# A reordered head, and float32 rows added by GpSimd's indirect transfers for nine batches of the last level of a graph layer on Trainium2

## The chip, the cores and the metric

One Trainium2 chip, one of its cores. The metric is the device time of one execution in microseconds; of several executions the median is given. The profile is of one execution, taken by the hardware profiler.

## The reference

A layer norm with a rectifier, one message-passing layer over a graph, and a residual. There are 12500 nodes with 64 features and 212500 edges that are sorted by destination; the hidden width is 128.

```python
    h = jnp.maximum(_layernorm(x, axis=-1), 0.0)
    ...
        edge_in = jnp.concatenate([h[row], h[col], dist], axis=1)
        e = jax.nn.silu(edge_in @ eW1 + eb1)
        e = jax.nn.silu(e @ eW2 + eb2)
        agg = jax.ops.segment_sum(e, row, num_segments=h.shape[0])
        node_in = jnp.concatenate([h, agg], axis=1)
        out = jax.nn.silu(node_in @ nW1 + nb1) @ nW2 + nb2
```

`row` is the source of an edge (and the node that it is summed into), `col` its destination, `dist` its weight. The layer's output is added to x.

## The kernel before, in words

A node is l * 100 + b: l is its place (0 to 124), b its bucket (0 to 99). The first edge matrix is split: A holds h times the part for the source, B the part for the destination, so the first layer of an edge is A[source] + B[destination] + weight and bias. A and B are kept as two float32r halves side by side (256 numbers, `ta` and `tb` in DRAM), whose sum is the float32 row.

**Sorting.** The edges come in 208 blocks of 1024 in the order of destination. For each block DVE counts the edges by source bucket (`oh` L457, `each` L465, `terms` L481, `rank` L483, and `pick` L446, which selects rows of B), TensorE forms the rows Q = B[destination] + weight + bias (`qp` L531), ACT copies them with the source's place in its bucket (`qs`, L543 and L546), and GpSimd sends them by eight indirect transfers a block (L553) to their bucket and rank in the DRAM buffer `q`. Slots of `q` that may stay empty are filled with zeros beforehand on ACT's queue (L123).

**Levels.** The ranks are cut into 14 levels; a level begins when the block that fills it has been sent. A level has 25 batches of four buckets, and a batch has one or two steps of 512 slots; the last level has one step a batch. A batch's Q rows come by one load on SP (`qt`, L612; four buffers), its A rows by another (`a`, L632; three buffers, 512 KB).

One step passes through these stages, in a loop over `turn` that takes a different step at each place: `one` (L719, DVE: which node of its bucket a slot belongs to), `lr` and `oneT` (L668 on TensorE and L673 on ACT: its transpose), `pt` (L685: transposes of the Q rows; L692: eight products of oneT with A's halves, which pick A's row for each slot and add it), `e` (L701, ACT), `p` (L730, L736, L740: second layer), `seg` (L753: sum by node), and the addition to `aggT` (L762 or L764, DVE). Between the stages, at the places marked None (hooks), other work is let in: sorting of later blocks, making of A, the node stage.

**Level 0** makes A itself, in a generator `made_a` that is advanced one part at each hook, three batches ahead: load of h (`hrl`, L642), product (L288, ACT L292, DVE L295), store to `ta` (L647), and h's share of the node stage: `zo` (L651), `zos` (L654, ACT; one buffer), stored to `own` (L656).

**Last level.** Once a batch's sum is complete, the node stage for its buckets is interleaved with the steps of later batches: x rows (`xr`, L335, the addition on GpSimd), `misc` (L348, on top of the own share), `zs` (L349), `o` (L358), `os` (L361), and the own share of the next batch copied into `misc` (L363).

**Order.** TensorE, DVE, ACT and SP run their instructions in the order of the program; GpSimd's order is planned by the scheduler. The head (the first 30 us) is a list of calls to generators: `src0` turns the sources of the first half into place and bucket, `lists_` the destinations into window starts, `rows_` and `made[0]` the norm and the first rows of B, `firstw` the edge weights.

Of the kernel before, what the change touches and what calls it, by code (L numbers as in the profile page):

```python
# [28 lines left out]
F32 = mybir.dt.float32  # L29
# [3 lines left out]
I32 = mybir.dt.int32  # L33
# [6 lines left out]
P = 128  # L40
# [39 lines left out]
def tile_gnn(ctx: ExitStack, tc: tile.TileContext, x, src, dst, ew, eW1, eb1, eW2, eb2, nW1, nb1, nW2, nb2, out):  # L80
# [194 lines left out]

    tb0 = dram.tile([P * NE, 2 * H], F32, name="tb0")
    tb00 = dram.tile([P * G, 2 * H], F32, name="tb00")
    ta_buckets, tb_buckets = (t.rearrange("(l b) f -> l b f", b=NB) for t in (ta, tb))

    def product(s, hr, ps, tag, to):  # L280
# [93 lines left out]
    with work:  # L374
# [38 lines left out]
        def load(s):  # L413

            if s < nblocks:
                p, g = s // 2, s % 2
                win = wins[p % NW]
                table, end = (tb0, NE * P) if s < EARLY else (tb, NB * P)
                if s < 2 * FIRST_PAIRS:
                    table, end = tb00, G * P  # L420
                assert s < EARLY or len(done_b) == NB // G
                if g == 0:
                    of = identb[:, p % HB :: HB][:, :, None].to_broadcast([P, 2, HB])
                    nc.scalar.copy(sels[p % NW].rearrange("p (a m) -> p a m", a=2), of)
# [180 lines left out]
        def fetch(i):  # L605
            if i >= len(batches):
                return
            c, B, n = batches[i]
            assert not any(pending[: c + 1])
            at = B * G * ROWS + G * (ENDS[c] - n * P)  # L610
            qt = ld2.tile([P, G * most, W], F32, name="qt")
            ins = nc.sync.dma_start(  # L612
                qt[:, : G * n, :].rearrange("p j w -> p (j w)"),
                q[at : at + G * n * P, :].rearrange("(p j) w -> p (j w)", p=P),
            ).ins
            for later in range(c + 1, len(LEVELS)):
                tc.declare_no_dep(ins, group=f"rows{later}", reason="these ranks were full before")
            tc.add_manual_dep(ins, last_rows[LEVELS[c][1] - 1].name, AFTER)
            tc.add_to_no_dep_group("loads", ins)
            batch[c, B] = [qt, None, None]  # L620

        def fetch_a(i):

            if i >= len(batches):
                return
            c, B, n = batches[i]
            a = lda.tile([P, G, 2 * H], F32, name="a")
            if c == 0:
                making[B] = made_a(B, a)
                next(making[B])  # L630
            else:
                nc.sync.dma_start(a, ta_buckets[:, B * G : B * G + G])  # L632
            batch[c, B][1] = a
# [3 lines left out]
        def made_a(B, a):  # L637

            while B not in done_b:
                next(feed)  # L640
            hr = late.tile([P, G // 2, P], F32, name="hrl")
            nc.sync.dma_start(hr, hd[:, B * G // 2 : (B + 1) * G // 2, :])  # L642
            for _ in range(3):
                yield
            yield from product(0, hr, mm, "mm", a.rearrange("p g (k h) -> p g k h", k=2))
            yield
            nc.sync.dma_start(ta_buckets[:, B * G : B * G + G], a)  # L647
            zo = [mm.tile([P, G // 2, L], F32, name="zo", tag="mm") for _ in range(2)]
            for h in range(2):
                half = slice(h * D, (h + 1) * D)  # L650
                nc.tensor.matmul(zo[h], w1n[half, :], hr[half, :, :L], start=True, stop=True)  # L651
            zos = late1.tile([P, G * L], F32, name="zos")
            for h in range(2):
                nc.scalar.copy(zos.rearrange("p (i a l) -> p i a l", a=2, l=L)[:, :, h], zo[h])  # L654
            yield
            nc.sync.dma_start(own[:, B, :], zos)  # L656
            yield

        def of(k):
# [2 lines left out]
            return batch[c, B], [((g * G + t) % n * G + (g * G + t) // n, (g * G + t) // n) for t in range(G)]  # L662

        def s_turn(k):
            tops = st[k]["one"].rearrange("p g l -> p (g l)").bitcast(BF16)
            lr = mm.tile([L, G, P], F32, name="lr", tag="mm")
            for t in range(G):
                nc.tensor.matmul(lr[:, t, :], tops[:, 2 * t * L + 1 : 2 * (t + 1) * L : 2], identb, start=True, stop=True)  # L668
            st[k]["lr"] = lr

        def s_one_t(k):
            oneT = wk.tile([L, G, P], F32, name="oneT")
            nc.scalar.copy(halves(oneT), st[k].pop("lr"))  # L673
            st[k]["oneT"] = oneT

        def s_pt(k):

            (qt, a, _), tiles = of(k)
            c, B, _, _ = steps[k]
            for _ in making.pop(B, ()) if c == 0 else ():  # L680
                pass
            oneT = st[k].pop("oneT")
            pt = mm.tile([P, G, P], F32, name="pt", tag="mm")
            for t, (j, _) in enumerate(tiles):
                nc.tensor.matmul(  # L685
                    pt[:, t, :], qt[:, j, :H], ident, is_transpose=True, start=t == 0, stop=False, skip_group_check=True
                )
            for b, same in itertools.groupby(range(G), lambda t: tiles[t][1]):
                same = list(same)
                cols = slice(same[0], same[-1] + 1)  # L690
                for i in range(2):
                    nc.tensor.matmul(  # L692
                        pt[:, cols, :],
                        halves(a[:L, b, i * H : (i + 1) * H]),
                        halves(oneT[:, cols, :]),
                        start=False,
                        stop=i == 1,
                        skip_group_check=True,
                    )
            e1 = wk.tile([P, G, P], F32, name="e1")  # L700
            nc.scalar.activation(e1, pt, AF.Silu)  # L701
# [257 lines left out]
        with listing:  # L959
# [5 lines left out]
            consts, zone_ = tables(), zones()  # L965
            next(rows_)
            next(consts)
            next(lists_)
            limits()
            next(rows_)  # L970
            next(firstw)
            next(lists_)
            nc.scalar.copy(halves(three2[:, 0, :]), three)
            nc.gpsimd.tensor_tensor(three2[:, 1, :], three, three2[:, 0, :], op=OP.subtract)
            last_rows_of(wins[0])
# [2 lines left out]
                last_rows_of(win)  # L978
            for xs in xss:
                nc.gpsimd.memset(xs, 0.0)  # L980
            next(rows_)
            next(src0)
            next(lists_)
            next(made[0])
            for part_ in (src0, made[0], firstw, made[0], made[0], lists_, src0, consts):
                next(part_)
            load_rows(0)
            load(0)
            load_sources(1)
            load(1)  # L990
            for part_ in (lists_, zone_):
                next(part_)
# [29 lines left out]
        aggT = aggp.tile([P, NB, L], F32, name="aggT")  # L1022
        late = work.enter_context(tc.tile_pool(name="late", bufs=3))
        late1 = work.enter_context(tc.tile_pool(name="late1", bufs=1))
        ld2 = work.enter_context(tc.tile_pool(name="ld2", bufs=NQ))
        lda = work.enter_context(tc.tile_pool(name="lda", bufs=NA))
        ones_ = work.enter_context(tc.tile_pool(name="ones", bufs=NO))
# [202 lines left out]
```

## Time and profile before

| | |
|---|---|
| median of 3 runs | 3503.77 us (3501.37 to 3517.39) |
| the profiled execution | 3483.84 us |
| its span | 3482.0 us |
| mean granted TensorE clock | 0.802 |
| first send (L553) | at 27.02 us |
| level 0, first and last fetch | 283.64 and 526.44 us |
| busy: TensorE, DVE, ACT, GpSimd | 67%, 53%, 40%, 47% |

A row of the timeline gives start, duration, engine, line, operation, output<-inputs, shape, number of instructions, and in brackets how long the engine had been idle before and what ended it. PE is TensorE, PEld its weight loads, POOL is GpSimd, and SPq the queue of SP. In the groups of the page, the numbers behind the count are busy time, mean nanoseconds of one, and idle time ahead of them by releaser. The chain of waits has start, duration, engine and line only.

### The profile page before, as it was taken

Reading aid. Unit: us, or ns where it says so; the run is one execution under the profiler, and the core shown is the slowest. Engines: PE = TensorE matmul, PEld = TensorE weight load, DVE = VectorE, ACT = ScalarE, POOL = GpSimd, SP = SyncE. Lnnn points to the kernel's source line nnn. Section 1 sums busy time; section 2 is a strip of 40 time slices with the busy share of each in tenths; the row PEclk is TensorE's granted clock in tenths of the full one; section 3 lists DMA queues with packets and bytes.
Section 4 is the critical chain, followed back from the end, with each engine's and each line's share of the span. In section 5 each row is a group of like instructions: output and inputs, shape, how many; then the busy total and the mean of one; then the engine's idle time right before and its main releaser. Section 6 shows DMA issues by size and latency. Waiting matters only on the chain. (4 is left out here: it accounts for less than half of the span.)

```text
span 3482.0 us, 47653 instructions
## 1 busy us (share of the span) xinstructions
PE 2344.1 (67%) x16730; PEld 2160.0 (62%) x16772; DVE 1842.7 (53%) x2884; ACT 1380.4 (40%) x3001; POOL 1641.7 (47%) x1724
## 2 busy tenths in 40 slices
PE   4445777735776567656765676767777767776799
PEld 3234666634665567556755666766676766766797
DVE  8775566554546445544454444455554554555443
ACT  3223444322444344334433444434443434443454
POOL 7665555465445544444445444444444544444401
PEclk7555778866887788778877888888888888888899
DMA  4344566654544345445553445455555655555586
GB/s 153 136 162 165 174 203 213 196 165 144 175 147 155 130 137 169 137 133 157 170 169 130 146 163 161 145 160 165 171 169 152 186 163 163 172 175 158 164 260 188
DMA packets 243744, 572.56 MB, mean 164 GB/s; under 512 B 47069, under 2 KB 106133, under 8 KB 243191
## 3 DMA queue, kind: packets, MB, share of 16 engines
q1 hardware_dynamic: 160308, 393.28, 36.6%
q0 software_dynamic: 53408, 122.68, 9.8%
q10 hardware_dynamic: 29782, 53.47, 4.8%
q8 instruction: 136, 2.23, 0.3%
q14 instruction: 110, 0.90, 0.1%
HBM read 349.93 MB, written 219.27 MB: 163 GB/s over the span
## 5 line engine op out<-in xcount | busy, mean ns | idle before, releaser
L553 POOL DMA_INDIRECT q<-qs,to x1661 | 1604.8, 966 | 1672.4 <-ACT qs L546 1174.1
L692 PE MATMUL pt<-oneT,a 125*128 125x128 f32 (+1 forms) x2800 | 491.9, 320 | 621.3 <-ACT oneT L673 518.8
L692 PEld LDWEIGHTS pt<-oneT,a 125*128 125x128 f32 x2800 | 415.3, 222 | 667.8 <-ACT oneT L673 552.5
L701 ACT ACTIVATE e<-pt 128x512 f32<-128x512 f32 x450 | 268.9, 598 | 1087.3 <-PE pt L692 374.4
L764 DVE TENSOR_TENSOR aggT<-aggT,seg 128x500 f32<-128x500 f32 x324 | 218.3, 674 | 876.0 <-remote 266.0
L736 PE MATMUL p<-w,e 128*128 128x128 f32 x3600 | 597.1, 319 | 0.0
L753 PE MATMUL seg<-one,e 128*128 128x125 f32 x3592 | 557.8, 303 | 51.1 <-DVE aggT L764 32.8
L736 PEld LDWEIGHTS p<-w,e 128*128 128x128 f32 x3600 | 548.1, 230 | 24.3 <-issue 22.4
L753 PEld LDWEIGHTS seg<-one,e 128*128 128x128 f32 x3592 | 498.1, 213 | 69.7 <-DVE aggT L764 37.9
L531 PE MATMUL qp<-win,pick 128*128 128x256 f32 x1664 | 379.4, 363 | 101.0 <-issue 49.2
L719 DVE TENSOR_TENSOR one<-misc,qt 128x500 f32<-128x500 f32 x425 | 286.0, 673 | 288.7 <-remote 75.4
L531 PEld LDWEIGHTS qp<-win,pick 128*128 128x128 f32 x1664 | 299.6, 248 | 184.1 <-issue 85.0
L543 ACT COPY qs<-qp 128x512 f32<-128x512 f32 x418 | 245.5, 588 | 406.4 <-issue 147.2
L740 ACT ACTIVATE e<-p 128x512 f32<-128x512 f32 x450 | 268.9, 598 | 278.8 <-remote 151.4
L465 DVE TENSOR_REDUCE each<-oh 128x100 bf16<-128x800 bf16 x208 | 318.3, 1530 | 7.2
L673 ACT CAST oneT<-lr 125x512 fp32r<-125x512 f32 x450 | 263.8, 586 | 101.8 <-remote 49.2
L685 PE MATMUL pt<-ident,qt 128*128 128x128 f32 x1800 | 284.8, 282 | 11.4 <-issue 5.0
L481 DVE TENSOR_TENSOR terms<-oh,misc 128x800 f32<-128x800 bf16 x208 | 203.6, 979 | 128.2 <-remote 95.4
L730 ACT COPY p<-b2f 128x512 f32<-128x512 f32 x450 | 267.1, 593 | 0.0
L685 PEld LDWEIGHTS pt<-ident,qt 128*128 128x128 f32 x1800 | 220.6, 147 | 28.5 <-issue 12.9
L483 DVE TENSOR_REDUCE rank<-terms 128x8 f32<-128x864 f32 x208 | 219.0, 1053 | 7.2
L668 PEld LDWEIGHTS <-one 128*125 128x125 bf16 x1800 | 197.5, 161 | 28.4 <-issue 27.0
(163 smaller groups left out, 1736.7 us busy)
## 6 DMA issues: line engine op xcount, KB each, us to landing
a<-ta SPq DMA_DIRECT2D x325, 512.0 KB
qt<-q SPq DMA_DIRECT2D x250, 288.0 KB
qt<-q SPq DMA_DIRECT2D x100, 576.0 KB
q<-zeros ACTq DMA_DIRECT2D x25, 1080.0 KB
q<-qs,to POOLq DMA_INDIRECT x1661
win<-tb SPq DMA_DIRECT2D x208, 120.0 KB
tb<-got SPq DMA_DIRECT2D x30, 512.0 KB
q<-zeros ACTq DMA_DIRECT2D x20, 720.0 KB
```

Source lines behind the costliest of these rows:

```text
L465: nc.vector.tensor_reduce(each, oh.rearrange("p t b -> p b t"), AX.X, OP.add)
L531: nc.tensor.matmul(qp[:, t % 2, :k], halves(pick[:, t * P : (t + 1) * P]), halves(win[:, :k, v]), start=v == 0, stop=v == 1,)
L553: ins = nc.gpsimd.indirect_dma_start(out=q[:], out_offset=bass.IndirectOffsetOnAxis(ap=to[:k, j : j + 1], axis=0), in_=qs[:k, t % 2, a, :] ...
L673: nc.scalar.copy(halves(oneT), st[k].pop("lr"))
L685: nc.tensor.matmul(pt[:, t, :], qt[:, j, :H], ident, is_transpose=True, start=t == 0, stop=False, skip_group_check=True)
L692: nc.tensor.matmul(pt[:, cols, :], halves(a[:L, b, i * H : (i + 1) * H]), halves(oneT[:, cols, :]), start=False, stop=i == 1, skip_group_c ...
L701: nc.scalar.activation(e1, pt, AF.Silu)
L719: nc.vector.tensor_tensor(one.rearrange("p (b j) l -> p b j l", j=n), (spots if c < len(LEVELS) - 1 else nodes1)[:, None, None, :].to_broa ...
L730: nc.scalar.copy(p2, b2f)
L736: nc.tensor.matmul(p2[:, t, :], e1[:, t, :], w2, start=False, stop=t == G - 1, skip_group_check=True)
L740: nc.scalar.activation(e2, p2, AF.Silu)
L753: nc.tensor.matmul(item[2][:, b, :], e2[:, t, :], one[:, t, :], start=j < G, stop=j >= G * (n - 1))
```

## The change

Lines are counted in the new kernel here, so some stand up to 37 lines further down.

**Level 0.** Behind the own store, `made_a` gets one more part: the float32 sum of A's halves is formed on DVE in `a32` and stored to a new DRAM buffer `ta32`. `a32` takes the same single buffer as `zos`.

**Last level.** For the batches whose number is a multiple of three (0, 3, ... 24: 9 of 25), A's rows come from `ta32`: GpSimd works out the row number of each slot's source (an empty slot takes some row, and is not summed), and four indirect transfers, one for each of the batch's tiles, add the rows of 128 slots onto Q's rows in `qt`. For these batches there is no load of A, no `lr`, no `oneT`, and no product L692; `pt` is the transposes alone.

**Head.** Same work, other order: the norm first, then the sources of the first half, the first rows of B, the destinations. The loads of the second half's sources are issued ahead of the first window's.

```diff
+            if picked_up(c, B):
+                near = wk.tile([P, G], F32, name="near")
+                nc.gpsimd.tensor_scalar(near, qt[:, :G, H], 1.0, float(NB), op0=OP.max, op1=OP.mult)
+                row_of = wk.tile([P, G], I32, name="row_of")
+                nc.gpsimd.tensor_tensor(near, near, shift[:, B * G : B * G + G], op=OP.add)
+                nc.gpsimd.tensor_copy(row_of, near)
+                for t in range(G):
+                    nc.gpsimd.indirect_dma_start(
+                        out=qt[:, t, :H],
+                        out_offset=None,
+                        in_=ta32[:],
+                        in_offset=bass.IndirectOffsetOnAxis(ap=row_of[:, t : t + 1], axis=0),
+                        compute_op=OP.add,
+                    )
+
+        def picked_up(c, B):
+
+            return c == len(LEVELS) - 1 and B % 3 == 0
...
             c, B, n = batches[i]
+            if picked_up(c, B):
+                return
             a = lda.tile([P, G, 2 * H], F32, name="a")
...
-            zos = late1.tile([P, G * L], F32, name="zos")
+            zos = late1.tile([P, G * H], F32, name="zos", tag="zos")[:, : G * L]
...
             nc.sync.dma_start(own[:, B, :], zos)
             yield
+            a32 = late1.tile([P, G, H], F32, name="a32", tag="zos")
+            nc.vector.tensor_tensor(a32, a[:, :, :H], a[:, :, H:], op=OP.add)
+            nc.sync.dma_start(ta32.rearrange("(l b) f -> l b f", b=NB)[:, B * G : B * G + G, :], a32)
+            yield
...
         def s_turn(k):
+            if picked_up(*steps[k][:2]):
+                return
...
         def s_one_t(k):
+            if picked_up(*steps[k][:2]):
+                return
...
-            for b, same in itertools.groupby(range(G), lambda t: tiles[t][1]):
+            for b, same in itertools.groupby(range(G), lambda t: tiles[t][1]) if oneT is not None else ():
...
-            next(lists_)
             limits()
             next(rows_)
+            next(rows_)
+            next(src0)
+            next(made[0])
+            next(lists_)
             next(firstw)
-            next(lists_)
...
-            next(rows_)
-            next(src0)
-            next(lists_)
             next(made[0])
-            for part_ in (src0, made[0], firstw, made[0], made[0], lists_, src0, consts):
+            for part_ in (src0, lists_, lists_, made[0], made[0], firstw, src0, lists_, consts):
                 next(part_)
             load_rows(0)
+            load_sources(1)
             load(0)
-            load_sources(1)
...
+        shift = aggp.tile([P, NB], F32, name="shift")
+        nc.vector.tensor_scalar(shift, nodes1[:, :NB], -float(NB + 1), None, op0=OP.add)
```

DVE's order in level 0 after the change, where the first three batches' `zos` have been stored (a tile's number tells its instances apart; `a_2170`, `a_2175` and `a_2180` are the A rows of batches 0, 1 and 2):

```order
L486 TENSOR_SCALAR to_2324<-rank_2322 128x8
L754 TENSOR_TENSOR one_2350<-misc_211,qt_2173 128x500
L458 TENSOR_TENSOR oh_2377<-misc_211,bkt_178 128x800
L466 TENSOR_REDUCE each_2379<-oh_2377 128x100
L680 TENSOR_TENSOR a32_2383<-a_2170 128x512
L680 TENSOR_TENSOR a32_2386<-a_2175 128x512
L680 TENSOR_TENSOR a32_2389<-a_2180 128x512
L447 TENSOR_SCALAR pick_2252<-bc_2381,same_148,extra0_152 128x512
L477 TENSOR_TENSOR alike_2428<-bkt_178 128x64
```

Before, `pick_2252` stood right behind `each`; the three additions now stand between them. The other 22 stand singly.

GpSimd's order at the end of the sends, after the change (the first two rows are the last sends of the program, then come batches 0, 3 and 6 of the last level):

```order
L554 DMA q_62<-qs_28132,to_28090 230528x144 x3
L554 DMA q_62<-qs_28177,to_28090 230528x144 x2
L624 TENSOR_SCALAR near_28618<-qt_28616 128x4
L626 TENSOR_TENSOR near_28618<-near_28618,shift_1030 128x4
L627 COPY row_of_28620<-near_28618 128x4
L629 DMA qt_28616<-ta32_175,row_of_28620 128x128 x4
L624 TENSOR_SCALAR near_28711<-qt_28709 128x4
L626 TENSOR_TENSOR near_28711<-near_28711,shift_1030 128x4
L627 COPY row_of_28713<-near_28711 128x4
L629 DMA qt_28709<-ta32_175,row_of_28713 128x128 x4
L336 TENSOR_TENSOR xr_28745<-xr_28745,nb2b_185 125x256
L336 TENSOR_TENSOR xr_28791<-xr_28791,nb2b_185 125x256
```

Before, the `xr` additions followed the last sends; two batches' gathers now stand ahead of them, and from there on one batch's gathers stand ahead of every three additions.

ACT's order in the head, of before and then of after (`x0` is the squared norm input, `var` the root, `sf` the sources, `got` the first rows of B):

```order
L787 ACTIVATE x0_77<-cen_217 128x256
L875 COPY firstf_221<-dstR_79 128x1
L792 ACTIVATE var_229<-var_229 128x4
L914 COPY ew00_127<-ew0_126 8x512
L973 COPY three2_125<-three_124 3x128
L896 COPY sf_80<-srcR_78 104x1024
L886 COPY base_i_179<-lot_236 1x64
L806 COPY hr_260<-ht_257 128x256
L292 COPY got_265<-ab_266 128x2x128
```

```order
L822 ACTIVATE x0_77<-cen_218 128x256
L827 ACTIVATE var_226<-var_226 128x4
L931 COPY sf_80<-srcR_78 104x1024
L841 COPY hr_236<-ht_233 128x256
L910 COPY firstf_238<-dstR_79 128x1
L949 COPY ew00_127<-ew0_126 8x512
L1010 COPY three2_125<-three_124 3x128
L293 COPY got_256<-ab_257 128x2x128
L293 COPY got_256<-ab_260 128x2x128
```

The root, the sources and `hr` moved ahead of the copies that wait for the destinations and the edge weights.

More of the change, by code (lines that the diff above doesn't have):

```diff
@@ L277, in tile_gnn @@
     tb00 = dram.tile([P * G, 2 * H], F32, name="tb00")
+    ta32 = dram.tile([P * NB, H], F32, name="ta32")
     ta_buckets, tb_buckets = (t.rearrange("(l b) f -> l b f", b=NB) for t in (ta, tb))
@@ L681, in s_pt @@
                 pass
-            oneT = st[k].pop("oneT")
+            oneT = st[k].pop("oneT", None)
             pt = mm.tile([P, G, P], F32, name="pt", tag="mm")
@@ L685, in s_pt @@
                 nc.tensor.matmul(
-                    pt[:, t, :], qt[:, j, :H], ident, is_transpose=True, start=t == 0, stop=False, skip_group_check=True
+                    pt[:, t, :],
+                    qt[:, j, :H],
+                    ident,
+                    is_transpose=True,
+                    start=t == 0,
+                    stop=oneT is None and t == G - 1,
+                    skip_group_check=True,
                 )
-            for b, same in itertools.groupby(range(G), lambda t: tiles[t][1]):
+            for b, same in itertools.groupby(range(G), lambda t: tiles[t][1]) if oneT is not None else ():
                 same = list(same)
```

## Prediction

> **What bounds the kernel now.** I read the page first, then the windows of 100 us, then the chain of waits, and the timeline at the three places that the change touches. The first rows are of the page.
>
> ```profile
> PE 2344.1 (67%) x16730; PEld 2160.0 (62%) x16772; DVE 1842.7 (53%) x2884; ACT 1380.4 (40%) x3001; POOL 1641.7 (47%) x1724
> ...
> L553 POOL DMA_INDIRECT q<-qs,to x1661 | 1604.8, 966 | 1672.4 <-ACT qs L546 1174.1
> ...
> L764 DVE TENSOR_TENSOR aggT<-aggT,seg 128x500 f32<-128x500 f32 x324 | 218.3, 674 | 876.0 <-remote 266.0
> ```
>
> No engine is full over the span, so the stages have to be read apart. The windows show, for each stretch, the busy microseconds of PE, its weight loads, DVE, ACT and POOL, then the granted clock and the share of the DMA engines.
>
> ```profile
> 300.00:400.00 100.00, 73.42 (x425) 61.77 (x423) 52.83 (x85) 39.00 (x98) 50.50 (x54) 0.70 0.50 171
> 700.00:800.00 100.00, 32.62 (x157) 26.24 (x158) 49.59 (x76) 17.75 (x47) 65.14 (x68) 0.57 0.43 139
> 3300.00:3400.00 100.00, 99.92 (x870) 94.53 (x870) 40.39 (x67) 57.84 (x107) 8.77 (x12) 1.00 0.82 257
> 3340.00:3350.00 10.00, 10.00 (x97) 10.00 (x96) 4.14 (x6) 6.04 (x13) 1.46 (x2) 1.00 1.01 339
> ```
>
> There are three kinds of stage. In level 0 (300 to 400 us) all engines are between 39% and 73%: they wait for each other in program order. At 700 to 800 us PE is at 33%, waiting for rows. In the last level, from about 3340 us, PE has no idle time and runs at the full granted clock; there a microsecond of PE removed can be a microsecond of time. The chain of waits is PE alone there; one step of it, 5.20 us, is
>
> ```profile
> 3453.93 0.94 PE seg L753 x8
> 3454.88 0.44 PE pt L685 x4
> 3455.31 0.84 PE pt L692 x8
> 3456.16 0.89 PE misc L348 x2
> 3457.05 0.89 PE p L736 x8
> 3457.94 0.96 PE o L358 x8
> 3458.90 0.24 PE lr L668 x4
> ```
>
> **The change, part by part: the last level.** For 9 of 25 batches `pt L692` (0.84) and `lr L668` (0.24) go: 1.08 us each, 9.7 us at most. But the `misc L348` behind them needs DVE's sum of the seg just made. At the end of the span, where neither pt nor lr stands between, the timeline shows how much of the gap remains:
>
> ```profile
> 3463.95 1.11 PE L753 MATMUL seg<-one,e 128*128 128x125 f32 x8
> ...
> 3465.85 0.69 PE L348 MATMUL misc<-aggT,w1g 128*128 128x500 f32 x1 [0.79 <-DVE aggT L764]
> ```
>
> From seg to misc it is 1.90 us there and 2.23 us (3453.93 to 3456.16) in the normal step. So of the 0.84 only 0.33 is gained and the rest becomes PE's wait for DVE; the 0.24 of lr stands elsewhere and is gained whole: 0.57 per batch, about 5 us for nine. The matching removals on ACT (nine `oneT` copies) and SP (nine loads) are worth nothing, as neither ends the chain.
>
> Against it stands the new chain: fetch of qt, three small POOL operations, four gathers, landing, then PE's transposes. How much time there is between a fetch and its transposes:
>
> ```profile
> 4.99 0.53 POOL L170 TENSOR_SCALAR low<-nodes 128x100 f32<-128x100 f32 x1
> ...
> 3328.26 2.47 SPq L612 DMA_DIRECT2D qt<-q  x2
> ...
> 3337.22 0.32 SPq L612 DMA_DIRECT2D qt<-q  x1
> ...
> 3338.43 0.90 SPq L132 DMA_DIRECT2D xr<-in_x_dram  x2
> ...
> 3339.99 0.60 PE L685 MATMUL pt<-ident,qt 128*128 128x128 f32 x4
> ...
> 3343.20 0.73 POOL L335 TENSOR_TENSOR xr<-xr,nb2b 125x256 f32<-125x256 f32 x1 [46.00 <-DMA xr<-in_x_dram]
> ...
> 3350.19 0.60 PE L685 MATMUL pt<-ident,qt 128*128 128x128 f32 x4
> ```
>
> For batch 0 it is 3328.26 to 3339.99, 11.7 us; for batch 3, 3337.22 to 3350.19, 13.0 us. From there a step takes 5.2 us instead of 3.4 (the 10.2 us between these two transposes are three steps), and a fetch goes four steps ahead or more, so later batches have about 18 us. What has to fit: the landing of the fetch, bounded by the xr load's 4.8 us (3338.43 to 3343.20); three small operations, at most 0.5 us each by POOL's first row; four gathers, priced by the nearest POOL row, the sends' 0.97 us and the 0.30 us between two sends (row below), 4.8 us; and the last landing, 2 to 4.8 us. Sum 12.7 to 15.9 us with these, or 10 us with a fetch that lands in 3. Batch 0 stalls 0 to 4 us, batch 3 0 to 3, later ones not. I take 1.5 us for both together: the stage gives 5 − 1.5 = 3.5 us (range +4 lost to 9.7 gained). POOL now does batches 0 and 3 ahead of its first xr addition, which moves these by about 8 us; three xr buffers hold three steps, 15.6 us, so this cover is enough.
>
> The Trainium skill ("DMA: Bandwidth & Descriptors", Anatomy of one DMA) gives a transfer of GpSimd's about 2.0 us fixed plus its bytes over 436 GB/s. By that, a 64 KB gather lands in an estimated 2.2 us, batch 0 would stall by less than 1 us, and the gain would be about 4.5; no run so far shows such a gather.
>
> **Level 0.** Here 25 additions on DVE (128x512) and 25 stores of 256 KB come in, and the addition's output shares one buffer with `zos`: it can start only when the own store has landed, and the next `zos` copy only when the new store has. The addition is priced by the aggT row, 0.67 us (128x500): 25 of them are 17 us of DVE work, which is half idle. The waits cost more. The first three batches are made together, and in the new DVE order their three additions stand in a row ahead of a pick:
>
> ```profile
> 315.41 0.64 ACT L654 COPY zos<-zo 128x250 f32<-128x250 f32 x2 [3.33 <-DMA own<-zos]
> ...
> 318.17 0.64 ACT L654 COPY zos<-zo 128x250 f32<-128x250 f32 x2 [2.12 <-DMA own<-zos]
> ...
> 319.21 0.75 DVE L446 SCALAR_TENSOR_TENSOR pick<-bc,same,extra 128x512 fp32r<-128x512 f32 x1 [2.52 <-PE bc L410]
> ...
> 321.43 1.16 PE L531 MATMUL qp<-win,pick 128*128 128x256 f32 x4
> ...
> 329.06 0.96 POOL L553 DMA_INDIRECT q<-qs,to  x1 [0.30 <-issue]
> ...
> 331.69 0.60 ACT L701 ACTIVATE e<-pt 128x512 f32<-128x512 f32 x1 [5.42 <-remote]
> ...
> 333.38 0.96 POOL L553 DMA_INDIRECT q<-qs,to  x1 [3.37 <-ACT zos L654]
> ```
>
> The first two rows show what a store's landing is worth to the copy behind it: 2.12 to 3.33 us. The third zos ends at 318.81; with 2.7 us for a landing the additions end at 322.2, 325.6 and 329.0, and the pick moves from 319.21 to there, 9.8 us. Behind it wait PE's qp at 321.43 and all that PE does after it; on SP the three new stores hold up the fetch and the load behind them equally. Part of it is absorbed: the sends ended at 330.02 and POOL then stood idle 3.37 us, and ACT stood 5.42 us ahead of e. With qp at 331 instead of 321 (and the next qp at 336.5 instead of 327.4) the next round of sends begins 4.6 us later if ACT's 5.42 us cover what they can, and 7 to 9.8 us later if they don't. I take 7.
>
> The other 22 come singly. Two of them:
>
> ```profile
> 385.83 0.32 SPq L656 DMA_DIRECT2D own<-zos  x1
> ...
> 390.62 0.75 DVE L295 TENSOR_TENSOR a<-ab,a 128x256 fp32r<-128x256 f32 x2 [3.70 <-ACT a L292]
> ...
> 552.08 1.21 SPq L656 DMA_DIRECT2D own<-zos  x1
> 552.17 0.75 DVE L446 SCALAR_TENSOR_TENSOR pick<-bc,same,extra 128x512 fp32r<-128x512 f32 x1
> ...
> 552.97 0.73 PE L531 MATMUL qp<-win,pick 128*128 128x256 f32 x4
> ```
>
> The addition ends 2.7 + 0.67 = 3.4 us after its own store's issue. After 385.83 that falls into DVE's 3.70 us of waiting: nothing lost. After 552.08 it ends at 555.5, the pick moves by 3.3 us, and PE's qp, which waits for the pick, by as much. Walking all 22 in this way, 17 cost nothing or a few tenths, and five 2 to 3.3 us: 12 us if nothing absorbs them, 0 if POOL's idle time between its rounds of eight sends (2 to 6 us each) does. I take 7. Level 0 costs 7 + 7 = 14 us (range 4.6 to 30; the upper end is 9.8 + 12 and as much again as PE loses in restarting behind each wait). These engines run in program order and the sends come out of the same stream, so a delay here is carried to the levels behind it.
>
> **The head.** Rows of the first 27 us:
>
> ```profile
> 8.32 0.19 ACT L875 CAST firstf<-dstR 128x1 f32<-128x1 int32 x1 [2.28 <-DMA dstR<-in_dst_dram]
> 8.42 0.20 ACT L792 ACTIVATE var<-var 128x4 f32<-128x4 f32 x1
> ...
> 24.85 1.04 ACT L896 CAST sf<-srcR 104x1024 f32<-104x1024 int32 x1 [6.08 <-DMA srcR<-in_src_dram]
> ...
> 27.02 1.28 POOL L553 DMA_INDIRECT q<-qs,to  x1 [7.05 <-ACT qs L546]
> ```
>
> The root at 8.42 stood 1.5 us behind a copy that waited for a load; now it goes first. The second half's load is issued earlier, so ACT's 6.08 us of waiting ahead of the copies for the first send shrink. I take 2.5 us off the first send at 27.02; between 0 (something else, the rank at DVE, is late next) and 4. The added shift tile is one small operation: nothing.
>
> **Sum.** +14 − 2.5 − 3.5 = +8 us on the profiled execution, 3483.84 to about 3492. That execution lies 19.9 us under the median of the runs, 3503.77; the same 8 us put the median at **3512 us**.
>
> **Rivals.**
> - **The waits of level 0 are hidden.** For it: DVE is idle half of 300 to 400 us, POOL waits after each round. Against it: qp follows the pick by 2 us in both rows above. Level 0 then costs 0 to 4, the sum is about −6 + 2 = −4: 3500 us. Not slower.
> - **They are exposed in full and restart PE slowly.** This ends slower. Its place is the pick behind an addition; its price 9.8 + 12 = 22 us, and half as much again in PE's restarts, 30 in all; it decides from the point at which qp moves by more than POOL's idle time ahead of a round (3.4 us at 333.38). 30 − 6 = +24: 3528 us.
> - **The gathers come late at every picked batch.** If each lands before the next begins, four take 4 × (0.97 + 4.8) = 23 us, more than the 15.6 us between picked batches: 8 us at each of nine, some 70 us, less what is gained: about 3580 us. For it: the DMA share is 1.01 at 3340 us. Against it: sends follow each other at 0.30 us without waiting for landings. The Trainium skill ("DMA: Bandwidth & Descriptors", Issuing engines are not separate DMA queues) says that all transfers share the same 16 engines whoever issued them; that speaks for lateness just there, though the picked batches load 256 KB in place of 512.
> - **The last level gives nothing**, because misc waits for DVE in any case: the 0.33 and 0.24 are lost, and the sum is +13, 3517 us.
>
> **How the numbers follow.** Forecast (sum between 0 and +16) 0.50, hidden 0.20, exposed 0.20, late gathers 0.04, last level worth nothing 0.06. The range 3493 to 3536 leaves out the late gathers and the ends of hidden and exposed. A measurement of this kernel can tell about 0.5% (17.5 us) from no change: faster by more than that 0.06 (the good end of hidden with all 9.7 us of the last level), slower 0.26 (most of exposed, the late gathers, the last level's worse half), the same 0.68.
>
> **What would show it.** In level 0: the three additions in a row with a DMA wait each, and the pick near 329 in place of 319. At single batches: additions whose wait names the own store, with PE's qp behind. In the last level: misc L348 waiting for aggT about 0.5 us in picked steps, and waits for a DMA ahead of the transposes of batches 0 and 3 only. In the head: the first send near 24.5. It would be wrong if sends in level 0 keep their rounds in spite of late picks, or if transposes wait for gathers from batch 6 on.

## The result, and the profile after

The changed kernel takes 3528.6 us (median of 11 runs, 3501.55 to 3546.31), the kernel before in the same comparison 3501.85 us (11 runs, 3494.71 to 3520.56): a ratio of 1.0063, 95% interval 1.0037 to 1.0089. (The ratio is not the quotient of the two medians, which is 1.0076; the same holds for the ratios further down.) By the ratio it is slower by about 22 us, by the medians by 27. The profiled execution took 3507.76 us, 23.9 more than that of before.

The page of the changed kernel shows no engine much busier than before:

```profile
PE 2358.1 (67%) x16622; PEld 2169.6 (62%) x16664; DVE 1856.3 (53%) x2910; ACT 1375.8 (39%) x2992; POOL 1706.7 (49%) x1787
```

DVE has 13.6 us more, GpSimd 65 us more; neither bounds the span. So the stretches have to be compared. Four marks cut both traces: the starts of the 161st and of the 321st send (blocks 20 and 40; between them lies level 0), the first fetch of the last level, and the end.

| us | before | changed | difference |
|---|---|---|---|
| start to 161st send | 272.9 | 273.15 | +0.25 |
| 161st to 321st send (level 0) | 293.1 | 312.5 | +19.4 |
| to the first fetch of the last level | 2762.2 | 2764.8 | +2.6 |
| last level to the end | 153.7 | 155.5 | +1.8 |

**Level 0** has nearly all of it. The timeline of the changed kernel where the first three batches are made (the profile drops digits from names, so `a<-a` at L680 is the addition into `a32`, and `ta<-a` at L681 the store to `ta32`):

```profile
322.51 0.69 DVE L680 TENSOR_TENSOR a<-a 128x512 f32<-128x512 f32 x1 [4.42 <-DMA own<-zos]
...
322.93 1.16 PE L532 MATMUL qp<-win,pick 128*128 128x256 f32 x4
...
323.23 5.91 SPq L681 DMA_DIRECT2D ta<-a  x3
...
325.30 0.69 DVE L680 TENSOR_TENSOR a<-a 128x512 f32<-128x512 f32 x1 [2.10 <-DMA ta<-a]
...
328.10 0.69 DVE L680 TENSOR_TENSOR a<-a 128x512 f32<-128x512 f32 x1 [2.10 <-DMA ta<-a]
328.71 0.75 DVE L447 SCALAR_TENSOR_TENSOR pick<-bc,same,extra 128x512 fp32r<-128x512 f32 x1
...
329.67 0.44 SPq L663 DMA_DIRECT2D hrl<-hd  x1
...
333.13 1.23 PE L289 MATMUL ab<-w,hrl 64*128 64x128 f32 x8 [8.40 <-DMA hrl<-hd]
...
336.81 1.16 PE L532 MATMUL qp<-win,pick 128*128 128x256 f32 x4
...
339.01 0.96 POOL L554 DMA_INDIRECT q<-qs,to  x1 [6.86 <-ACT qs L547]
```

The three additions end at 323.2, 326.0 and 328.8, each behind a landing, and the pick stands at 328.71 instead of 319.21. GpSimd's next round of sends begins at 339.01 instead of 333.38. Between the pick and the sends stands one more wait: TensorE waits 8.40 us for a load of h (`hrl`). SP issues that load at 329.67, behind the three new stores, and the last of these could only go when the third addition had been made. In the kernel before, the load went at 320.45, TensorE did not wait for it, and the products of this pick (`qp`, eight in two groups for each pick) began at 327.43 instead of 336.81:

```profile
320.45 0.43 SPq L642 DMA_DIRECT2D hrl<-hd  x1
...
323.75 1.23 PE L288 MATMUL ab<-w,hrl 64*128 64x128 f32 x8 [0.53 <-issue]
...
327.43 1.16 PE L531 MATMUL qp<-win,pick 128*128 128x256 f32 x4
```

The pick was ready at 329.46, the load landed later, and on TensorE `qp` stands behind the product L289; so here the way from the additions to the sends goes over SP's queue, and not over the pick. The `qp` at 322.93 is the second group of the pick before, and didn't wait. At the single batches the additions go on waiting:

```profile
352.85 0.34 SPq L677 DMA_DIRECT2D own<-zos  x1
354.98 0.69 DVE L680 TENSOR_TENSOR a<-a 128x512 f32<-128x512 f32 x1 [4.90 <-DMA own<-zos]
...
355.71 0.75 DVE L447 SCALAR_TENSOR_TENSOR pick<-bc,same,extra 128x512 fp32r<-128x512 f32 x1
...
367.49 0.32 SPq L677 DMA_DIRECT2D own<-zos  x1
369.56 0.69 DVE L680 TENSOR_TENSOR a<-a 128x512 f32<-128x512 f32 x1 [7.58 <-DMA own<-zos]
```

The landing itself takes 2.1 us (352.85 to 354.98), but DVE had been idle 4.90 and 7.58 us: in program order it reaches the addition before the own store is even issued, so it waits for ACT's copy, SP's issue and the landing in turn. The group of the 25 additions, busy 17.4 us, gives the sum of idle time ahead of them and its causes:

```profile
L680 DVE TENSOR_TENSOR a<-a 128x512 f32<-128x512 f32 x25 | 17.4, 694 | 78.1 <-DMA own<-zos 59.8 <-ACT a L293 5.9 <-ACT qs L544 4.3
```

**The last level**, batch 0. GpSimd starts on the landed rows at 3356.00, 5.6 us after the fetch was issued; a gather takes 1.57 us where a send takes 0.97; TensorE (the last three rows) waits three times.

```profile
3350.44 5.87 SPq L613 DMA_DIRECT2D qt<-q  x3
...
3356.00 0.24 POOL L624 TENSOR_SCALAR near<-qt 128x4 f32<-128x4 f32 x1 [38.91 <-PE pt L714]
...
3358.00 1.67 POOL L629 DMA_INDIRECT qt<-ta,row_of  x1 [0.86 <-PE lr L695]
...
3363.83 1.55 POOL L629 DMA_INDIRECT qt<-ta,row_of  x1 [0.30 <-issue]
...
3362.87 0.33 PE L714 MATMUL pt<-ident,qt 128*128 128x128 f32 x1 [0.83 <-DMA qt<-ta,row_of]
3365.78 0.58 PE L714 MATMUL pt<-ident,qt 128*128 128x128 f32 x2 [2.59 <-DMA qt<-ta,row_of]
3367.29 0.48 PE L714 MATMUL pt<-ident,qt 128*128 128x128 f32 x1 [0.92 <-DMA qt<-ta,row_of]
```

That is 0.83 + 2.59 + 0.92 = 4.3 us; batch 3 waits 0.87 us once. From batch 6 on there is no wait for a gather, and a picked step looks as follows: `misc` follows the transposes after 0.35 us of waiting for the sum, and `lr` and `pt L727` are missing.

```profile
3393.11 0.60 PE L714 MATMUL pt<-ident,qt 128*128 128x128 f32 x4
3394.06 1.11 PE L349 MATMUL misc<-aggT,w1g 128*128 128x500 f32 x2 [0.35 <-DVE aggT L799]
3395.01 1.05 PE L771 MATMUL p<-w,e 128*128 128x128 f32 x8
```

**The head**: the root and the sources go earlier, the first send only at 25.35 (before 27.02), and TensorE now waits for the first window's load:

```profile
6.96 0.20 ACT L827 ACTIVATE var<-var 128x4 f32<-128x4 f32 x1 [0.89 <-DVE var L826]
7.07 1.03 ACT L931 CAST sf<-srcR 104x1024 f32<-104x1024 int32 x1
...
23.09 2.05 PE L532 MATMUL qp<-win,pick 128*128 128x256 f32 x8 [4.16 <-DMA win<-tb]
...
25.35 1.75 POOL L554 DMA_INDIRECT q<-qs,to  x1 [3.65 <-ACT qs L547]
```

At the 33rd send both stand at 76.4 and 76.5 us: what was gained is gone. (In the traces further down, those of e9 and e10 aside, the 33rd send stands between 73.5 and 76.6 us, whichever the head, so one pair of traces can't say more.)

### The profile page after: what moved, and what is told of

Read it like the earlier page. It is cut to its first block, busy times and chain, and to the rows that moved or that the text cites. A ratio compares the mean times of both kernels' runs of the same rounds, so it can differ in the third digit from the quotient of the medians.

```text
span 3505.9 us, 47597 instructions
## 1 busy us (share of the span) xinstructions
PE 2358.1 (67%) x16622; PEld 2169.6 (62%) x16664; DVE 1856.3 (53%) x2910; ACT 1375.8 (39%) x2992; POOL 1706.7 (49%) x1787
## 4 chain that ended last, share of the span: by engine, by line
PE 47%; another core or an unknown queue 18%; ACT 11%; issue 8%; DVE 5%; DMA 2%; POOL 1%; SPq 0%; ACTq 0%; DVEq 0%; POOLq 0%
PE p L771 11%; PE pt L727 10%; PE seg L788 10%; PE qp L532 5%; PE pt L714 4%; PE lr L695 3%; ACT oneT L702 2%; ACT e L736 2%; ACT e L775 2%; ACT p L765 2%; ACT qs L544 1%; PE bc L411 1%; DVE aggT L799 1%; POOL q L554 1%
## 5 line engine op out<-in xcount | busy, mean ns | idle before, releaser
L727 PE MATMUL pt<-oneT,a 125*128 125x128 f32 (+1 forms) x2728 | 491.0, 325 | 598.6 <-ACT oneT L702 494.6
L727 PEld LDWEIGHTS pt<-oneT,a 125*128 125x128 f32 x2728 | 415.2, 227 | 646.4 <-ACT oneT L702 529.9
L771 PE MATMUL p<-w,e 128*128 128x128 f32 x3600 | 605.5, 323 | 0.0
L771 PEld LDWEIGHTS p<-w,e 128*128 128x128 f32 x3600 | 555.7, 233 | 26.0 <-issue 23.0
L754 DVE TENSOR_TENSOR one<-misc,qt 128x500 f32<-128x500 f32 x425 | 286.2, 674 | 260.8 <-PE seg L788 73.0
L482 DVE TENSOR_TENSOR terms<-oh,misc 128x800 f32<-128x800 bf16 x208 | 203.8, 980 | 97.0 <-remote 56.7
```

The lines of the kernel that those rows point to most:

```text
L727: nc.tensor.matmul(pt[:, cols, :], halves(a[:L, b, i * H : (i + 1) * H]), halves(oneT[:, cols, :]), start=False, stop=i == 1, skip_group_c ...
L771: nc.tensor.matmul(p2[:, t, :], e1[:, t, :], w2, start=False, stop=t == G - 1, skip_group_check=True)
```

## The experiments

**Theory:** DVE's wait ahead of each addition, in program order with the pick behind it, costs the 19.4 us. **Rivals:** the work of additions and stores; ACT's wait, since the next `zos` needs the new store's landing; the last level or the head. A further rival has no run of its own: SP's queue, where the new store waits for the addition and holds up the loads behind it. The chips differ in speed (before takes 2303 us on one, called fast here, and 3448 to 3503 us on three, called slow), so every ratio is to the kernel before on the same chip in the same comparison. "Level 0" is from the 161st to the 321st send and "last level" from its first fetch to the end, both from the one profiled execution.

| kernel | before, us | this, us | ratio (95%) | level 0, us | last level, us |
|---|---|---|---|---|---|
| before (trace) | | | | 293.1 | 153.7 |
| changed (first comparison) | 3501.85 | 3528.60 | 1.0063 (1.0037 to 1.0089) | 312.5 | 155.5 |
| e1, level 0's part alone | 3503.27 | 3526.66 | 1.0045 (1.0019 to 1.0071) | 319.3 | 153.8 |
| e2, own place | 3503.27 | 3517.01 | 1.0026 (1.0002 to 1.0050) | 295.5 | 155.3 |
| e3, head alone | 3503.27 | 3511.05 | 1.0028 (1.0002 to 1.0054) | 293.9 | 154.0 |
| e4, late picks | 3503.27 | 3522.99 | 1.0054 (1.0033 to 1.0076) | 308.8 | 150.2 |
| e5, DVE's wait only | 3455.69 | 3475.55 | 1.0055 (1.0026 to 1.0084) | 310.2 | 156.7 |
| e6, ACT's wait only | 3455.69 | 3454.92 | 0.9996 (0.9969 to 1.0023) | 281.6 | 157.2 |
| e7, own place, late picks, old head | 3455.69 | 3457.48 | 1.0009 (0.9986 to 1.0033) | 297.1 | 149.8 |
| e8, as e7, ten picks | 3455.69 | 3453.21 | 0.9994 (0.9971 to 1.0017) | 286.2 | 152.0 |
| e9, head alone again | 2303.08 | 2303.16 | 0.9999 (0.9989 to 1.0009) | 212.6 | 153.8 |
| e10, own place, late picks, new head | 2303.08 | 2310.88 | 1.0046 (1.0032 to 1.0059) | 215.5 | 150.4 |
| e11, changed again | 3448.09 | 3473.76 | 1.0067 (1.0044 to 1.0090) | 307.1 | 156.8 |
| e12, e7 again | 3448.09 | 3443.89 | 1.0003 (0.9977 to 1.0029) | 290.7 | 150.4 |

### Level 0's part alone, and without its waits

The edit of e1: nothing is picked up, and the head is the old one, so only the additions and stores are new.

```diff
-            return c == len(LEVELS) - 1 and B % 3 == 0
+            return False
```

> The kernel before with only level 0's part of the change (additions and stores of the float32 rows, in the buffer of zos); the head as before and no gathers, so the stored rows are not used. In the changed kernel the 321st send starts 19.6 us later than in the kernel before, at the end of level 0. If level 0 is what costs, this kernel shows the same there (+17 to +22 us) and its time is 0.4 to 0.8% above the kernel before. If the loss comes from the new head or from the last level, the send stands within 3 us of before and the time within 0.2%.

Level 0 took 319.3 us, 26.2 more than before; the 321st send stands 24.7 us later than before, above the 17 to 22 that were expected, and the time is 0.45% over. The loss comes with level 0's part alone; the last level is as before (153.8 us).

The edit of e2, the same additions and stores in another place (level 0 uses half of each `qt` buffer), with `zos` alone in its buffer again:

```diff
-            zos = late1.tile([P, G * H], F32, name="zos", tag="zos")[:, : G * L]
+            zos = late1.tile([P, G * L], F32, name="zos")
...
-            a32 = late1.tile([P, G, H], F32, name="a32", tag="zos")
+            a32 = batch[0, B][0][:, G:, :H]
```

> The changed kernel with one thing else: the float32 rows are written into the unused upper half of the batch's own qt buffer, so neither the addition waits for the own store nor the next zos for the new store; additions and stores are as many. If the waits for landings cost the 19.6 us, the 321st send comes 0 to 6 us after that of before, and the time falls to within 0.2% of the kernel before. If the additions' and stores' work itself costs (25 x 0.67 us on DVE, SP waiting behind them), 12 us or more stay.

Level 0 took 295.5 us, 2.4 more than before instead of 19.4. The group of the additions in this kernel has the same busy time and no idle time at all ahead of it:

```profile
L680 DVE TENSOR_TENSOR qt<-a 128x512 f32<-128x512 f32 x25 | 17.0, 686 | 0.0
```

So in these traces the work costs 2.4 us, and the sharing of a buffer the other 17. Single traces scatter, though: e7 and e8 below have the same level 0 and ran on one chip, and took 297.1 and 286.2 us for it. The total is still 0.26% over before, a little more than the 0.2% that was expected, with an interval that nearly touches 1; the last level (155.3 us) has 1.6 us of it, and the rest lies between, where executions of every kernel differ by tens of microseconds (the stretch from the 321st send to the last level was 2762 us in the trace of before, 2780 and 2801 in e3 and e1, which change nothing there).

### Whose wait

e5 puts a batch's zos and its float32 rows both into the batch's own place: DVE still waits, ACT does not. e6 puts the rows into the next batch's place: DVE no longer has to wait, but the next zos has. The edit of e5; e6 has `batch[0, min(B + 1, NB // G - 1)]` in its last line:

```diff
-            zos = late1.tile([P, G * H], F32, name="zos", tag="zos")[:, : G * L]
+            zos = batch[0, B][0][:, G:, :].rearrange("p j w -> p (j w)")[:, : G * L]
...
-            a32 = late1.tile([P, G, H], F32, name="a32", tag="zos")
+            a32 = batch[0, B][0][:, G:, :].rearrange("p j w -> p (j w)")[:, : G * H].rearrange("p (g h) -> p g h", g=G)
```

> The changed kernel with zos and the float32 rows of a batch both in the free upper half of that batch's own qt buffer: the addition still waits until the own store has landed, but the next batch's zos no longer waits for the new store. From the 161st to the 321st send it took 293.1 us before, 312.5 in the changed kernel, 295.5 without any such wait. If DVE's wait costs (the pick and what follows stand behind it), 306 to 313 us here; if ACT's wait for the new store costs, 295 to 300.

> The other half: a batch's zos goes to its own qt buffer's upper half, its float32 rows to that of the next batch, where the next zos follows. So from the fourth batch on the additions wait for no fresh store, and the next zos waits for the new store. From the 161st to the 321st send: 295 to 302 us if DVE's wait is what costs, 305 to 313 if ACT's is.

On the same chip level 0 took 310.2 us in e5, as expected of DVE's wait, and 281.6 in e6, even less than expected; the times are 1.0055 and 0.9996 of before, and their intervals don't overlap. The group of additions in e5 and then in e6:

```profile
L680 DVE TENSOR_TENSOR qt<-a 128x512 f32<-128x512 f32 x25 | 17.1, 692 | 73.4 <-DMA own<-qt 43.5 <-ACT e L775 10.3 <-ACT a L293 7.7
```

```profile
L680 DVE TENSOR_TENSOR qt<-a 128x512 f32<-128x512 f32 x25 | 17.0, 686 | 5.8 <-DMA own<-qt 5.8
```

Where DVE's 73.4 us of waiting fall away, the loss falls away. The 28.6 us between the two overstate it: waits of ACT that the trace puts down to no engine come to 48.6 us in e5's level 0, 47.4 in that of before, and only 22.3 in e6's. The table as a whole is firmer. The five traces with the waits (changed, e1, e4, e5, e11) have 307.1 to 319.3 us in level 0, the seven of slow chips without them (before, e2, e3, e6, e7, e8, e12) 281.6 to 297.1; the means are 20 us apart, and the groups don't overlap. So the additions' wait for a landing in a shared buffer is the cause. ACT's wait isn't needed for it: in e5 no copy into `zos` is seen to wait for a new store, and the loss is there. What that wait costs by itself was not measured, as the copies of e6 waited only 0.7 us for new stores.

Over which queue the wait reaches the sends is not separated. Wherever DVE waits, the new store on SP waits behind it, and the loads behind the store. At the first three additions it is SP's queue: the three stores hold it for 5.91 us in the changed kernel and TensorE waits 8.40 us for `hrl`; in e2 they hold it for 1.54 us and TensorE waits 3.90. In e5 the first three additions don't wait, and the 161st to the 193rd send took 56.7 us there and 56.5 in e6, so all of e5's loss lies at the other 22. In the changed kernel's chain of waits through level 0 stand nine additions: from five the chain goes on over the stores on SP, from three over DVE's next instruction, from one over ACT's next `zos`.

### The last level

> The changed kernel with gathers only for batches 6, 9, ... 24; batches 0 and 3 take their A rows by the load as before. From the first fetch of the last level to the end it took 1.7 us longer in the changed kernel than before. If the waits of PE for the gathers of batches 0 and 3 (4.3 and 0.9 us in the trace) eat the gain, this stretch is 3 to 4.5 us shorter than before now. If the removed work is hidden in any case, it stays within 1 us of before. The total stays near the changed kernel (0.4 to 0.7% over before), as level 0 is untouched.

```diff
-            return c == len(LEVELS) - 1 and B % 3 == 0
+            return c == len(LEVELS) - 1 and B % 3 == 0 and B >= 6
```

The last level took 150.2 us, 3.5 less than before and 5.3 less than in the changed kernel; no transposes wait for a gather. Seven picked batches save 0.5 us each; batches 0 and 3 had cost more than the whole gain. The total stayed near that of the changed kernel, as level 0 is the same.

> As the last, with every second batch from 6 on (6, 8, ... 24: ten instead of seven). A picked batch occupies GpSimd for about 9 us (four gathers of 1.86 us and three small operations), two steps take about 10 us. If the gain goes with the number, the last level is 5 us shorter than before (149 us); if GpSimd's time is the bound, transposes wait for gathers again and it is 151 us or more.

With ten picked batches (`B % 2 == 0 and B >= 6`, on top of e7) the last level took 152.0 us, more than the 149.8 with seven. TensorE waits for gathers again; two of the waits:

```profile
3365.91 0.33 PE L714 MATMUL pt<-ident,qt 128*128 128x128 f32 x1 [1.10 <-DMA qt<-ta,row_of]
...
3387.64 0.33 PE L714 MATMUL pt<-ident,qt 128*128 128x128 f32 x1 [1.15 <-DMA qt<-ta,row_of]
```

All of them come to 4.5 us in six waits, where seven picked batches had none. From the second of the ten on GpSimd has no idle time ahead of a picked batch, which fits the expectation that its time is the bound.

### The head

> The kernel before with the new head alone. In the changed kernel the first send came 1.7 us earlier and the 33rd as late as before. If the head's gain is lost at a wait that the head doesn't move, the first send is again 1.5 to 2 us early and the 33rd within 0.5 us of before, time within 0.2%. If the changed kernel's level 0 had only covered the gain, the 2 us are still there at the 161st send.

The first send came at 25.3 us, the 33rd at 73.9, 2.6 earlier than before and not within 0.5 as expected, the 161st at 273.0 (before 272.9); level 0 took 293.9. Three kernels with the old head had their first send at 24.98 (e1), 25.02 (e8) and 25.20 (e12), a fourth at 26.86 (e7): the 27.02 of before is one of two values that the old head gives, not its rule. The 0.28%, more than the expected 0.2%, had no place in the trace, so it was measured again:

> The new head alone a second time, the same kernel as in the first round, because its 0.28% over before (interval 0.02 to 0.54%) has no place in its trace: from the 161st send to the 321st and in the last level it is within 1 us of before. If the head costs something, 0.2 to 0.4% again; if that was scatter between executions, the ratio lies within 0.2% of 1 and the interval holds 1.

0.9999, with an interval of 0.1% to either side, on the fast chip. The head does nothing to the time that could be measured there.

### Both losses mended

> The old head, the float32 rows in the own qt buffer (no waits), gathers for batches 6, 9, ... 24 only. By the parts measured so far: level 0 +2.4 us (295.5 against 293.1), the last level 3.5 us shorter (150.2 against 153.7 us from its first fetch to the end). Sum -1 us: within 0.2% of the kernel before. If the new head costs something (its kernel alone was measured 0.28% over before, interval 0.02 to 0.54%), this one must lie below the one with the new head and rows in the own place (0.26% over before).

> Both losses mended, with the old head, a second time. The mended kernel with the new head was 0.46% over before on the fast chip (interval 0.32 to 0.59%), though its level 0 was 2.9 us longer and its last level 3.4 us shorter than the other kernel's there. If the head makes that, this one is within 0.2% of before; if the additions and stores cost somewhere behind level 0, it is 0.3 to 0.6% over on a fast chip again. On a slow chip: within 0.25%, which leaves it open.

e7 and e12 are one kernel, with `a32` as in e2, the condition of e4 and the old head: 1.0009 and 1.0003. The sum of the parts holds; nothing is gained that a measurement of this kernel can tell.

> The changed kernel with both losses mended and the new head kept: float32 rows in the own qt buffer, gathers for batches 6, 9, ... 24. By the parts: head 0, level 0 +2.4 us, last level -3.5 us: within 0.2% of before. The 161st to the 321st send 281 to 298 us, the last level 149 to 151 us. If the new head costs 0.28%, that much over before.

e10 is the same with the new head, and on a fast chip it was 0.46% over before, against both theories' sums. Its trace shows level 0 2.9 us longer than e9's on that chip, caught up by the 513th send (692.5 and 692.7 us), and the last level 3.4 us shorter; but its profiled execution, 2309.4 us, is the lowest of its five, and e9's, 2311.2 us, the highest of eleven, so the traces don't show the 8 us between the medians. As e9 has the same head and is level with before, they should come with the additions, the stores or the gathers; e12, meant to tell, ran on a slow chip. What costs e10 there stays open.

> The changed kernel again, because the chip of the last round ran the kernel before in 2303 us instead of 3503 or 3456, with hardly any of the waits that the trace cannot put down to an engine, and the first comparison was on a chip of the slower sort. If the loss is the additions' waits for landings, it does not depend on those: the 161st to the 321st send takes 15 to 25 us longer than the kernel without them on the same sort of chip (212.6 us on the fast one, 293.1 on the slow one), 0.6 to 1.0% of the fast one's time, 0.4 to 0.8% of the slow one's. If they only hurt together with the other waits, it is under 5 us on a fast chip.

The changed kernel again, on a slow chip: 1.0067, level 0 307.1 us. The first result repeats; what it would be on a fast chip wasn't measured. On the same chip e12, with the waits, the early gathers and the new head taken out, has 1.0003 and 290.7 us, 16.4 less.

## Why the prediction went as it did, point by point

- **The first three additions: the size came out, the path was another.** Forecast ends 322.2, 325.6 and 329.0, measured 323.2, 326.0 and 328.8; the pick at 328.71. From the 161st to the 193rd send the changed kernel took 65.9 us, before 60.5: 5.4 us were passed on, where 7 were taken and 4.6 was the lower bound. But the `qp` at 321.43, which the forecast moved together with the pick, belongs to the pick before (`qp` products come eight to a pick, in program order), and it did not move with this one: it stands at 322.93 in the changed kernel, ahead of the pick. The pick's own `qp` stood at 327.43, 8.2 us behind it. In the row at 552.17 it is the same: that pick's `qp` is at 556.99, not at 552.97. So "qp follows the pick by 2 us", which counted against the rival of hidden waits, was a misreading. What ended last was TensorE's wait for `hrl`, 8.40 us, behind the stores on SP; the forecast names that hold-up in half a sentence and gives it no size. That 5.4 fell between 4.6 and 7 is luck.
- **The other 22: the step that failed.** "12 us if nothing absorbs them, 0 if POOL's idle time between its rounds of eight sends (2 to 6 us each) does. I take 7." Nothing absorbed them: 19.4 − 5.4 = 14.0 us in the changed kernel, 20.8 in e1, 11.5 in e4. GpSimd's idle time was no cover, since its rounds begin when ACT's copies of `qp` are there: its waits for these (`qs` L546, now L547) grew in level 0 from 74.5 to 98.9 us. The row that was read as cover, at 390.62, was right for its batch: at the same place after the change (400.04) DVE waits 4.05 us where it had waited 3.70. But 17 such batches of 22 were counted as free or nearly so, and DVE stood idle ahead of 20 of the 22, for 69.5 us in all (78.1 with the first three). The loads behind the stores on SP were not priced here either.
- **The last level: a term was mis-sized.** Forecast 5 us of gain and 1.5 us of stalls; measured seven times 0.5 us (e4) against 0.57 a batch, and stalls of 4.3 + 0.9 us at batches 0 and 3. The forecast's rows add up to 13.1 to 15.9 us for the new chain, not 12.7 to 15.9, and to 11.3, not 10, with a fetch that lands in 3. Batch 0 took 16.9: 5.6 to the start of the small operations (4.8 at most was forecast), 2.0 for these (1.5), 7.4 for the gathers (4.8), 1.9 to the last transpose. The gathers were priced at the sends' 0.97 us and took 1.57 each on average; they are the largest error. The stall at batch 0 lies just past the forecast's bound of 4. The Trainium skill ("DMA: Bandwidth & Descriptors", Anatomy of one DMA) gave an estimated 2.2 us for a gather's landing; here 1.9 us passed from the end of the last gather of batch 0 (3365.38) to its transpose (3367.29), and 3.5 from its start (3363.83), so the estimate agrees only if it is counted from the end of issuing. The stall came mainly from issuing, 7.4 us for the four.
- **The head: a term that was nothing.** The 2.5 us were read off one execution whose first send was 2 us late of its own; in the new order qp waits 4.16 us for the window's load, which now goes behind the sources. The forecast's lower bound, 0, was the right value.
- **The sum.** +8 was taken, with 0 to +16 as the band of the forecast; the trace gives +0.25 + 19.4 + 2.6 + 1.8 = 24 us. By the forecast's own measure of 0.5% this is slower, to which it had given 0.26. The median, 3528.6, lies in the stated range of 3493 to 3536 because that range also takes in the sum of the rival "exposed in full". That rival gave +24 and is what happened, though by another sum: it had 30 in level 0, 8 of them for restarts of PE, for which there was no row, less 6 for the head and the last level; measured were 19.4 in level 0 and 2 us lost at the two ends. That the number is the same is luck. The late gathers at every batch did not come. The last level gave nothing, but because of the stalls at its first two batches; `misc`, waiting for DVE, did not eat the gain (e4).

## What to carry to other kernels

A buffer shared with a store puts the landing into the program order of the engine that writes it next: ask what stands behind that write on its engine, and behind the write's own store on the queue that issues it, not how long the write takes. Idle time of an engine covers a delay only if the delayed chain is not the one that the engine is idle for. Before a delay is moved from one row to the next, make sure that the second row reads what the first one writes, and not an earlier instance of the same name. An operation that the trace doesn't show should be priced by issue and landing apart, and a head start read off one execution needs a second one.

## What the runs showed of the hardware

The same program runs a third faster on one of the four chips of the experiments: before takes 2303 us there, and 3448 to 3503 on the three others. The sends cost the same on both (964 ns there, 966 in the trace of before). What differs most are waits that the trace puts down to no engine. In e3, on a slow chip, and in e9, the same kernel on the fast one, the window from 1500 to 1800 us:

```profile
1500.00:1800.00 300.00, 195.34 (x1463) 184.97 (x1466) 143.52 (x217) 121.76 (x256) 140.95 (x147) 0.82 0.49 159
```

```profile
1500.00:1800.00 300.00, 296.32 (x2731) 291.00 (x2730) 263.32 (x403) 198.94 (x436) 227.75 (x238) 1.00 0.87 278
```

TensorE is full there at the whole granted clock on the fast chip, and at 65% on the slow one. Two waits of e3, with their total, number and longest:

```profile
ACT e L701 <- remote: 411.7, 62, 20.6
DVE aggT L764 <- remote: 278.3, 67, 18.2
```

The trace of e9 has no wait of this kind; those of e3 come to 1197 us over all engines, and its span is 1191 us longer (waits of different engines can overlap, so the match proves nothing). What holds ACT and DVE there was not found. In the twelve traces of slow chips these waits come to between 1071 and 1231 us; that scatter is larger than any part of this change.
